# Masks on GpSimd, ReLU and sign on ScalarE, one VectorE operation for mask and maximum, in a planned graph-attention kernel

## The chip, the cores and the metric

The kernel runs on one core of a Trainium2 chip. A core has several engines that each work off their own instruction queue in order: TensorE (PE in the profile, its weight loads PEld), VectorE (DVE), ScalarE (ACT), GpSimd (POOL) and SyncE (SP); they meet through semaphores. 16 DMA engines move data between HBM and the on-chip memory SBUF; matmuls write to PSUM. The metric is the time of one execution in device microseconds (us).

## The reference, cut to what matters

```python
# x: 3327 x 1024, adj: 3327 x 3327 (0/1, symmetric, with the diagonal)
h = relu(layernorm(x))
f, g = h @ Wf + bf, h @ Wg + bg
e = relu(f @ g.T)
attention = softmax(where(adj > 0, e, -9e15), axis=1)
out = x + attention @ (h @ W + bW)
```

A node has about 16 neighbours and none has more than 37, so nearly all of the 3327 x 3327 scores are masked away.

## The kernel before, in words

The kernel never forms the whole score matrix. In its first part (to about 245 us) it normalises the rows of x and stores h in HBM (`hd`), makes one matrix A from Wf and Wg so that f·g of two nodes is (h A)·h', counts the neighbours of each node, lists them, and sorts the nodes by their number of neighbours. The second part, which the change touches, works through 26 tiles of 128 nodes, in the order `ORDER`. A tile of a given size gives each of its nodes the same number of neighbour slots (`CAPS`, 37 down to 11, 468 slots in all). A slot k of tile t is one row of 1024 floats for each of the 128 nodes, fetched from `hd` with an indirect DMA (512 KB) into one of 26 row buffers `G`.

The steps of a tile t have short names, which are the functions in the code:

- `L(t)`: fetch the lists of neighbours and the degree of the tile's nodes (POOL issues it). `G(t,k)`: fetch slot k (POOL). `H(t)`: fetch the tile's own h (POOL). `X`, `O`: add x to the result and scatter it to the output (POOL).
- `q`, `hT`, `hc`, `qc`, `fq`: transpose h, multiply with A on PE; ScalarE copies between PSUM and SBUF. The result `q` is 128 x 1026 wide; its column 1024 (`D`) is h·(Wf bg) plus a constant, the part of the score that the bias bg makes, here with its sign turned, since column D of `WgT` holds -bg (L899).
- `M(t)` (L1233): the mask: for 40 slots, -9e15 where the slot number is at or beyond the node's degree, else 0. One tensor_scalar of 128 x 40 on VectorE, into one of three buffers.
- `d(t,k)` (`dot`, L1258): multiply row k with q and sum it up: one score per node, one VectorE operation over 1024 elements.
- `S(t,c)` (`greatest`, L1265): for a chunk c of slots (tiles with more than 18 slots have two chunks, ten tiles do; 36 chunks in all): max(score, column D of q) plus the mask, in one scalar_tensor_tensor; then the negated maximum with a tensor_reduce into `nm`; for a second chunk also the minimum with the first chunk's `nm`.
- `E(t,c)`: exp(score + nm) with its sum, on ScalarE; `A(t)`: the factor that rescales the first chunk; `T`: the reciprocal of the sum (VectorE).
- `Y(t,c)`: scale row 0 (ScalarE). `s(t,k)`: row 0 += weight x row k on VectorE (L1313). For other slots, given by `SHARE`, `w(t,k)` scales the row on ScalarE (L1296) and `p(t,k)` adds it up on PE (L1300). `yt`, `yc`, `W`, `fo`, `rc`: transpose the weighted row on PE, multiply it with W, and copy the result out (L1316 to L1339).

The order of all these steps on every engine is fixed before the launch. `steps_of()` lists each step with its engine, two costs (how long it holds its engine, how long until its result is there) and the steps it must follow. `planned()` runs a list scheduler over that (`forward`), computes ranks backwards from the end (`backward`), adds random noise from `SEED` and `WIDE` to the ranks, repeats this 30 times and keeps the order with the least modelled end. The instructions are then issued in that order with no further reordering. So a change in one step's engine, cost or seed can move every other step. In this list a fetch holds POOL for 1.31 us, a dot holds VectorE for 1.148, an `s` step 1.205, the mask 0.16, and S 0.29 (first chunk) or 0.48 (second). A step of which several have an engine's turn is taken by least rank; a fetch also needs a free row buffer, which an earlier `s`, `p` or transpose has given back.

The list's dependence of `M(t)` on steps of tile t-3 is for the reuse of buffers; in the code the mask waits for the landing of `L(t)` and for S(t-3), which read the same mask buffer.

Of the kernel before, what the change touches and what calls it, by code (L numbers as in the profile page):

```python
# [12 lines left out]
AF = mybir.ActivationFunctionType  # L13
ALU = mybir.AluOpType
AX = mybir.AxisListType
# [23 lines left out]
TURNS = 6.0  # L39
ROWS = 26  # L40
PASSES = 30
SEED = 1
WIDE = 0.3
LAG = 2

# [283 lines left out]
def steps_of():  # L329

    steps = {}

    def add(engine, takes, lasts, name, *deps, **kw):
        steps[name] = Step(name, engine, takes, lasts, deps, **kw)

    chunks = [split(s) for s in ORDER]
    n = len(ORDER)
    add("DVE", 0.15, 0.2, ("fl", 0), at=265.0)
    for t, s in enumerate(ORDER):
        cap, ends = CAPS[s], chunks[t]  # L340
        add("POOL", 1.31, 1.31, ("L", t), ("M", t - 3), *(("G", t - 3, k) for k in range(CAPS[ORDER[t - 3]] if t > 2 else 0)))
        add("DMA", 0.4, 2.2, ("Ld", t), ("L", t))
        if t > 1:
            add("POOL", 1.31, 1.31, ("H", t), row=True)
            add("DMA", 1.33, 3.2, ("Hd", t), ("H", t))
            for g in range(2):
                add("PE", 0.44, 0.66, ("hT", t, g), ("Hd", t), ("hc", t - 1, g), ("hT", t, g - 1), frees=[("H", t)] * g)
            for g in range(2):
                add("ACT", 0.49, 0.6, ("hc", t, g), ("hT", t, g), *(("q", t - 1, i, j) for i in range(3) for j in range(QS)))
            for i in range(3):  # L350
                for j in range(QS):
                    add(
                        "PE", 4.66 / QS, 4.66 / QS + 0.2, ("q", t, i, j), ("hc", t, 0), ("hc", t, 1), ("fq", 3 * t + i),
                        ("q", t, i, j - 1),
                    )
                add(
                    "ACT", 0.4, 0.52, ("qc", t, i), ("q", t, i, QS - 1),
                    *(("d", t - 2, k) for k in range(CAPS[ORDER[t - 2]])), *(("S", t - 2, c) for c in range(2) if i == 2),
                )
                if 3 * t + i + 2 < 3 * n:  # L360
                    add("ACT", 0.38, 0.48, ("fq", 3 * t + i + 2), ("qc", t, i))
        used = [(op, t - 3, k) for op in "swY" for k in range(KM)]
        add("DVE", 0.16, 0.25, ("M", t), ("Ld", t), ("S", t - 3, 0), ("S", t - 3, 1), ("rc", t - 3, 0), ("rc", t - 3, 1), *used)
        if s < MORE:
            add("POOL", 1.31, 1.31, ("C", t), ("F", t - 1))
            add("DMA", 0.4, 2.5, ("Cd", t), ("C", t))
            add("DVE", 1.3, 1.4, ("F", t), ("Cd", t), *(("G", t - 1, k) for k in range(KL, CAPS[ORDER[t - 1]])))
        if t == n - 1:
            add("POOL", 1.31, 1.31, ("x", t), row=True)
            add("DMA", 1.33, 3.2, ("xd", t), ("x", t))  # L370
        summed, halves = [], ([], [])
        for c, (k0, k1) in enumerate(ends):
            last = c == len(ends) - 1
            for k in range(k0, k1):
                late = [("F", t)] if k >= KL else [("hc", 2, 1) if k < 6 else ("qc", 2, 1)] if t == 1 else []
                add("POOL", 1.31, 1.31, ("G", t, k), ("Ld", t), *late, row=True)
                add("DMA", 1.33, 3.2, ("Gd", t, k), ("G", t, k))
                add(
                    "DVE", 1.148, 1.32, ("d", t, k), ("Gd", t, k), *(("qc", t, i) for i in range(3)),
                    ("M", t), at=(256.0, 266.0)[t] if t < 2 else 0.0,  # L380
                )
            add("DVE", 0.48 if c else 0.29, 0.6 if c else 0.41, ("S", t, c), *(("d", t, k) for k in range(k0, k1)), ("M", t))
            if c:
                add("ACT", 0.28, 0.33, ("A", t), ("S", t, c))
            add("ACT", 0.48, 0.55, ("E", t, c), ("S", t, c), ("fl", t))
            if c:
                add("ACT", 1.05, 1.15, ("Y", t, c), ("A", t), *(("s", t, k) for k in range(1, k0)))
            else:
                add("ACT", 1.05, 1.15, ("Y", t, c), ("E", t, c))
            add("DVE", 0.25 * c + 0.11 * last + 0.01, 0.25 + 0.2 * c, ("T", t, c), ("E", t, c), *([("A", t)] if c else []))  # L390
            for k in range(max(k0, 1), k1):
                if k in on_tensor(t):
                    add("ACT", 1.05, 1.15, ("w", t, k), ("E", t, c))
                    add("PE", 0.873, 1.07, ("p", t, k), ("w", t, k), ("yc", t - 1, 0), ("yc", t - 1, 1), frees=[("G", t, k)])
                    summed.append(("p", t, k))
                elif t < n - 1:
                    add("DVE", 1.205, 1.29, ("s", t, k), ("E", t, c), ("Y", t, c), frees=[("G", t, k)])
                    summed.append(("s", t, k))
                else:
                    for g in range(2):  # L400
                        add("DVE", 0.66, 0.74, ("s", t, k, g), ("E", t, c), ("Y", t, c), ("s", t, k, g - 1), frees=[("G", t, k)] * g)
                        halves[g].append(("s", t, k, g))
        for o in range(2):
            add("ACT", 0.62, 0.72, ("fo", t, o), ("rc", t - 1, o), ("T", t, len(ends) - 1))
        for g in range(2):
            add(
                "PE", 0.44, 0.66, ("yt", t, g), *summed, *halves[g], ("Y", t, len(ends) - 1), ("yc", t - 1, 0), ("yc", t - 1, 1),
                ("yt", t, g - 1),
                frees=[("G", t, 0)] * g,
            )  # L410
        for g in range(2):
            add("ACT", 0.49, 0.6, ("yc", t, g), ("yt", t, g), *(("W", t - 1, o, j) for o in range(2) for j in range(WS)))
        for o in range(2):
            for j in range(WS):
                add(
                    "PE", 7.0 / WS, 7.0 / WS + 0.2, ("W", t, o, j), *(("yc", t, g) for g in range(2 * (j + 1) // WS)),
                    ("fo", t, o), ("W", t, o, j - 1),
                )
            if t < n - 1:
                add("ACT", 0.62, 0.72, ("rc", t, o), ("W", t, o, WS - 1), ("Od", t - 2))  # L420
            else:
                add("DVE", 0.6, 0.7, ("rc", t, o), ("W", t, o, WS - 1), ("Od", t - 2), ("xd", t), ("rc", t, o - 1), frees=[("x", t)] * o)
        if t < n - 1:
            add("POOL", 2.05, 2.05, ("X", t), ("rc", t, 0), ("rc", t, 1))
            add("DMA", 2.0, 4.5, ("Xd", t), ("X", t))
        add("POOL", 1.31, 1.31, ("O", t), ("Xd", t), ("rc", t, 0), ("rc", t, 1))
        add("DMA", 1.33, 3.2, ("Od", t), ("O", t))
    for step in steps.values():
        step.deps = [steps[d] for d in step.deps if d in steps]
        for d in step.deps:  # L430
            d.after.append(step)
    return list(steps.values())
# [147 lines left out]
def edge_path(ctx: ExitStack, tc: tile.TileContext, x, adj, Wf, bf, Wg, bg, W, bW, out, flag):  # L580
# [67 lines left out]
    with ExitStack() as part1:  # L648
# [212 lines left out]
        with tc.manual_schedule(engines={  # L861
# [34 lines left out]
            caps = c1.tile([P, NT], FP, name="caps")  # L896
            for j, cap in enumerate(CAPS):
                nc.gpsimd.memset(caps[:, j : j + 1], float(cap))
            nc.gpsimd.tensor_scalar(WgT[:, :, D], bgT, -1.0, None, op0=ALU.mult)  # L899
            load_adj(1)  # L900
            load_w(Wg, 0)
            load_w(Wg, 1)
# [265 lines left out]
    with tc.manual_schedule(engines={  # L1168
# [36 lines left out]
        def unit(of, t, c):  # L1205
            return of[2 * (t % 3) + c]
# [25 lines left out]

        def M(t):  # L1233
            degree = pis[t % 3].bitcast(FP)[:, KL : KL + 1]
            nc.vector.tensor_scalar(masks[t % 3], iotak, degree, NEG, op0=ALU.is_ge, op1=ALU.mult)

        def turned(t, g):
            for k in range(4):
# [25 lines left out]

        def greatest(t, c):  # L1265
            k0, k1 = chunks[t][c]
            sc, nm = scs[t % 3][:, k0:k1], unit(nms, t, c)
            nc.vector.scalar_tensor_tensor(  # L1268
                sc, sc, qs[t % 2][:, D : D + 1], masks[t % 3][:, k0:k1], op0=ALU.max, op1=ALU.add
            )  # L1270
            nc.vector.tensor_reduce(nm, sc, AX.X, ALU.max, negate=True)  # L1271
            if c:
                nc.vector.tensor_tensor(nm, nm, unit(nms, t, 0), op=ALU.min)

        def A(t):
            nc.scalar.activation(als[t % 3], unit(nms, t, 0), AF.Exp, bias=unit(nms, t, 1), scale=-1.0)
# [82 lines left out]
        def told(_):  # L1359
# [1 line left out]

        made = {
            "fl": told, "L": L, "H": H, "x": fetch_x, "C": C, "F": F, "G": fetch, "M": M, "hT": turned, "hc": hc, "q": third, "qc": qc,
            "fq": fq, "d": dot, "S": greatest, "A": A, "E": E, "Y": Y, "T": T, "w": w, "p": p, "s": s, "fo": fo, "yt": yt,
            "yc": yc, "W": project, "rc": rc, "X": X, "O": scatter,
        }
        plan = sorted(planned(ROWS, PASSES, SEED, WIDE)[1], key=lambda step: step[0])
# [45 lines left out]
```

## Time and profile before

| | us |
|---|---|
| median of 3 runs (1228.5 to 1233.57) | 1232.57 |
| the profiled execution | 1233.38 |
| its span, first to last instruction | 1231.6 |
| PE busy in the span | 1099.2 (89%) |
| VectorE busy | 1120.3 (91%) |
| ScalarE busy | 602.7 (49%) |
| GpSimd busy | 936.7 (76%) |
| mean granted TensorE clock | 0.963 of full |

The profile's groups name a line, an engine, the operation, what is written and read, the count, the busy time with the mean of one in ns, and the idle time of that engine just ahead of the group with what ended it. "issue" there is a gap in which the engine waited for nothing that the profile shows. A windows row gives each engine's busy time within a stretch of the span, with the number of instructions behind an x. A timeline row gives start, duration, engine, line and operation.

### The profile page before, as it was taken

How to read it: one execution, taken by the hardware profiler on the slowest of the kernel's cores; microseconds unless marked ns; L12 is line 12 of the kernel's file. 1: busy time of each engine (PE TensorE's matmuls, PEld its weight loads, DVE VectorE, ACT ScalarE, POOL GpSimd, SP SyncE). 2: the span in 40 equal slices, each digit the busy share in tenths (PEclk: the TensorE clock that was granted, in tenths of full speed). 3: DMA queues.
4: the chain of work that ended last, by engine and by line, in shares of the span. 5: the costliest groups of instructions: out<-in, count | busy, mean ns of one | idle time of the engine just before them, and what ended most of it. 6: DMA issues, size and time to landing. Idle time of an engine off the chain costs nothing. (4 is left out here: it accounts for less than half of the span.)

```text
span 1231.6 us, 14006 instructions
## 1 busy us (share of the span) xinstructions
PE 1099.2 (89%) x4508; PEld 697.5 (57%) x4508; DVE 1120.3 (91%) x2192; ACT 602.7 (49%) x924; POOL 936.7 (76%) x677
## 2 busy tenths in 40 slices
PE   2799990799939899999999999999899999999995
PEld 2566660466627466556655666665465656556553
DVE  5999998758898999998999999999999999999991
ACT  6899986324617355436452455443343333434240
POOL 8999996177676888878878778777887888787821
PEclk9899995799979999999999999999999999999998
DMA  9999999589788999989899899888998999998942
GB/s 370 420 396 397 393 359 324 191 313 350 270 257 281 329 314 315 319 285 339 302 342 308 307 306 320 279 286 299 317 294 288 311 310 321 283 316 256 324 118 54
DMA packets 101913, 374.43 MB, mean 304 GB/s; under 512 B 14859, under 2 KB 18602, under 8 KB 98631
## 3 DMA queue, kind: packets, MB, share of 16 engines
q0 software_dynamic: 79584, 286.77, 69.4%
q1 hardware_dynamic: 22246, 86.68, 18.7%
q8 instruction: 37, 0.61, 0.2%
q14 instruction: 46, 0.38, 0.1%
HBM read 344.11 MB, written 29.30 MB: 303 GB/s over the span
## 5 line engine op out<-in xcount | busy, mean ns | idle before, releaser
L639 POOL DMA_INDIRECT G<-hd,ps x454 | 567.4, 1250 | 159.2 <-issue 107.0
L1260 DVE CUSTOM_DVE_ANT_0 junk<-G,q 128x1024 bf16<-128x1024 f32 x468 | 563.9, 1224 | 34.0 <-DMA G<-hd,ps 19.2
L1328 PE MATMUL p_o<-W_sb,yT 128*128 128x512 f32 x832 | 365.8, 593 | 4.7 <-issue 3.1
L1313 DVE SCALAR_TENSOR_TENSOR G<-G,sc 128x1024 f32<-128x1024 f32 (+1 forms) x281 | 354.5, 1262 | 6.8 <-ACT G L1285 3.7
L1247 PE MATMUL p_q<-A_sb,hT 128*128 128x342 f32 x1152 | 350.5, 455 | 7.8 <-ACT p_q L1256 5.7
L1247 PEld LDWEIGHTS p_q<-A_sb,hT 128*128 128x128 f32 x1152 | 214.7, 191 | 116.4 <-issue 12.7
L1328 PEld LDWEIGHTS p_o<-W_sb,yT 128*128 128x128 f32 x832 | 155.1, 189 | 189.0 <-issue 180.9
L1300 PE MATMUL p_y<-ident,G 128*128 128x128 f32 x1552 | 190.1, 275 | 12.7 <-DVE G L1313 6.8
L1300 PEld LDWEIGHTS p_y<-ident,G 128*128 128x128 f32 x1552 | 175.0, 142 | 40.8 <-issue 15.3
L704 POOL TENSOR_TENSOR r<-r,iotaj 128x1664 f32<-128x1664 f32 (+3 forms) x50 | 183.9, 3750 | 3.9 <-ACT r L697 3.9
L1296 ACT ACTIVATE G<-G,sc 128x1024 f32<-128x1024 f32 x168 | 179.2, 1138 | 0.1
L837 PE MATMUL ps_A<-WgT,WfT 128*128 128x342 f32 x432 | 130.5, 461 | 1.6 <-ACT WfT L832 1.6
L767 DVE MAX8 cand<-r 128x8 f32<-128x208 f32 (+2 forms) x416 | 118.9, 360 | 4.0 <-POOL r L704 3.7
L1339 ACT ACTIVATE xp<-p_o,rs 128x512 f32<-128x512 f32 x50 | 34.2, 685 | 172.7 <-PE p_o L1328 131.5
L837 PEld LDWEIGHTS ps_A<-WgT,WfT 128*128 128x128 f32 x432 | 81.7, 193 | 42.1 <-issue 2.3
L697 ACT ACTIVATE r<-r 128x3327 f32<-128x3327 int32 (+3 forms) x27 | 77.3, 2865 | 10.2 <-DMA r<-in_adj_dram 10.2
L1253 ACT COPY q<-p_q 128x342 f32<-128x342 f32 x72 | 31.6, 443 | 103.0 <-PE p_q L1247 59.5
L1324 ACT COPY yT<-p_y 128x512 f32<-128x512 f32 x52 | 30.0, 587 | 71.6 <-PE p_y L1300 59.6
L1243 ACT COPY hT<-p_t 128x512 f32<-128x512 f32 x48 | 27.4, 585 | 74.4 <-PE p_t L1240 37.9
L639 POOL DMA_INDIRECT xp<-in_x_dram,perm x25 | 44.3, 1772 | 21.1 <-ACT xp L1339 14.4
L1281 ACT ACTIVATE sc<-sc,nm 128x10 f32<-128x10 f32 (+10 forms) x36 | 10.9, 304 | 94.4 <-DVE nm L1271 66.2
L1346 POOL DMA_INDIRECT out_dram<-xp,perm x25 | 32.8, 1310 | 31.1 <-DMA xp<-in_x_dram,perm 22.9
(148 smaller groups left out, 728.4 us busy)
## 6 DMA issues: line engine op xcount, KB each, us to landing
r<-in_adj_dram SPq DMA_DIRECT2D x24, 1663.5 KB, 12.8
xt<-in_x_dram SPq DMA_DIRECT2D x22, 512.0 KB, 13.6
hd<-xt SPq DMA_DIRECT2D x22, 512.0 KB, 10.5
G<-hd,ps POOLq DMA_INDIRECT x454
A_sb<-in_L_gnn_Wg_dram SPq DMA_DIRECT2D x8, 512.0 KB, 18.4
A_sb<-in_L_gnn_Wf_dram SPq DMA_DIRECT2D x8, 512.0 KB, 12.0
W_sb<-in_L_gnn_W_dram SPq DMA_DIRECT2D x8, 512.0 KB, 7.4
cd<-cand SPq DMA_DIRECT2D x25, 64.0 KB, 12.6
```

The lines of the kernel that those rows point to most:

```text
L639: return nc.gpsimd.indirect_dma_start(out=to, out_offset=None, in_=table, in_offset=bass.IndirectOffsetOnAxis(ap=idx, axis=0), **kw,)
L697: nc.scalar.activation(r[:n, b:e], a[:n, b:e], AF.Sign, accum_out=to)
L704: eng.tensor_mul(r[:n, b:e], r[:n, b:e], iotaj[:n, b:e])
L767: nc.vector.max(cands[t][:n, s * 8 : s * 8 + 8], r[:n, s * SW : min(N, (s + 1) * SW)])
L837: nc.tensor.matmul(ps[:, :QB], WfTs[c][:, k, :], WgT[:, k, o : o + QB], start=(k == 0), stop=(k == KD - 1))
L1247: nc.tensor.matmul(ps_q[(3 * t + i) % 2][:, :QB], hT[:, k, :], A_sb[:, k, i * QB : (i + 1) * QB], start=False, stop=(k == KD - 1), skip_gr ...
L1260: nc.vector.tensor_tensor_reduce(junks[k % 2], row(t, k), q[:, :D], 1.0, 0.0, op0=ALU.mult, op1=ALU.add, accum_out=scs[t % 3][:, k : k + 1],)
L1296: nc.scalar.activation(g, g, AF.Copy, scale=scs[t % 3][:, k : k + 1])
L1300: nc.tensor.matmul(ps_y[g][:, c, :], of[:, (4 * g + c) * P : (4 * g + c + 1) * P], ident, is_transpose=True, start=((t, g) not in begun an ...
L1313: nc.vector.scalar_tensor_tensor(y, row_k, scs[t % 3][:, k : k + 1], y, op0=ALU.mult, op1=ALU.add)
L1328: nc.tensor.matmul(ps_o[o], yT[:, k, :], W_sb[:, k, o * CB : (o + 1) * CB], start=False, stop=(k == KD - 1), skip_group_check=True,)
L1339: nc.scalar.activation(to, ps_o[o], AF.Copy, scale=rss[t % 3])
```

## The change

The mask moves to GpSimd's queue, with the same operation. The score's clamp is undone from S: a new step `R(t,c)` on ScalarE computes relu(score + column D of q) in place, for which column D of `WgT` holds +bg instead of -bg (all scores of a node differ from before by the same number, which softmax removes). S is then one tensor_tensor_reduce on VectorE: add the mask, write the sum, and take the maximum into `al` (first chunk) or `rs` (second chunk, where it starts from the first chunk's maximum in `al`). A new step `N(t,c)` on ScalarE writes the negated maximum to `nm`, which E and A read as before. The steps' list gets these engines, costs and dependences; the seed goes from 1 to 8, and the whole order of the second part is computed anew.

```diff
-SEED = 1
+SEED = 8
 ...
-                    *(("d", t - 2, k) for k in range(CAPS[ORDER[t - 2]])), *(("S", t - 2, c) for c in range(2) if i == 2),
+                    *(("d", t - 2, k) for k in range(CAPS[ORDER[t - 2]])), *(("R", t - 2, c) for c in range(2) if i == 2),
 ...
-        add("DVE", 0.16, 0.25, ("M", t), ("Ld", t), ("S", t - 3, 0), ("S", t - 3, 1), ("rc", t - 3, 0), ("rc", t - 3, 1), *used)
+        add("POOL", 0.2, 0.25, ("M", t), ("Ld", t), ("S", t - 3, 0), ("S", t - 3, 1), ("rc", t - 3, 0), ("rc", t - 3, 1), *used)
 ...
-            add("DVE", 0.48 if c else 0.29, 0.6 if c else 0.41, ("S", t, c), *(("d", t, k) for k in range(k0, k1)), ("M", t))
+            add("ACT", 0.2, 0.3, ("R", t, c), *(("d", t, k) for k in range(k0, k1)))
+            add("DVE", 0.22, 0.32, ("S", t, c), ("R", t, c), ("M", t), *([("S", t, 0)] if c else []))
+            add("ACT", 0.19, 0.28, ("N", t, c), ("S", t, c))
             if c:
-                add("ACT", 0.28, 0.33, ("A", t), ("S", t, c))
-            add("ACT", 0.48, 0.55, ("E", t, c), ("S", t, c), ("fl", t))
+                add("ACT", 0.28, 0.33, ("A", t), ("N", t, c), ("N", t, 0))
+            add("ACT", 0.48, 0.55, ("E", t, c), ("N", t, c), ("fl", t))
 ...
-            nc.gpsimd.tensor_scalar(WgT[:, :, D], bgT, -1.0, None, op0=ALU.mult)
+            nc.gpsimd.tensor_copy(WgT[:, :, D], bgT)
 ...
-            nc.vector.tensor_scalar(masks[t % 3], iotak, degree, NEG, op0=ALU.is_ge, op1=ALU.mult)
+            nc.gpsimd.tensor_scalar(masks[t % 3], iotak, degree, NEG, op0=ALU.is_ge, op1=ALU.mult)
 ...
         def greatest(t, c):
             k0, k1 = chunks[t][c]
-            sc, nm = scs[t % 3][:, k0:k1], unit(nms, t, c)
-            nc.vector.scalar_tensor_tensor(
-                sc, sc, qs[t % 2][:, D : D + 1], masks[t % 3][:, k0:k1], op0=ALU.max, op1=ALU.add
+            sc = scs[t % 3][:, k0:k1]
+            nc.vector.tensor_tensor_reduce(
+                sc, sc, masks[t % 3][:, k0:k1], 1.0, als[t % 3] if c else 0.0, op0=ALU.add, op1=ALU.max,
+                accum_out=(rss if c else als)[t % 3],
             )
-            nc.vector.tensor_reduce(nm, sc, AX.X, ALU.max, negate=True)
-            if c:
-                nc.vector.tensor_tensor(nm, nm, unit(nms, t, 0), op=ALU.min)
+
+        def negated(t, c):
+            nc.scalar.activation(unit(nms, t, c), (rss if c else als)[t % 3], AF.Copy, scale=-1.0)
+
+        def bounded(t, c):
+            k0, k1 = chunks[t][c]
+            sc = scs[t % 3][:, k0:k1]
+            nc.scalar.activation(sc, sc, AF.Relu, bias=qs[t % 2][:, D : D + 1])
```

More of the change, by code (lines that the diff above doesn't have):

```diff
@@ L1363, in edge_path @@
             "fl": told, "L": L, "H": H, "x": fetch_x, "C": C, "F": F, "G": fetch, "M": M, "hT": turned, "hc": hc, "q": third, "qc": qc,
-            "fq": fq, "d": dot, "S": greatest, "A": A, "E": E, "Y": Y, "T": T, "w": w, "p": p, "s": s, "fo": fo, "yt": yt,
+            "fq": fq, "d": dot, "R": bounded, "S": greatest, "N": negated, "A": A, "E": E, "Y": Y, "T": T, "w": w, "p": p, "s": s, "fo": fo, "yt": yt,
             "yc": yc, "W": project, "rc": rc, "X": X, "O": scatter,
```

## The prediction

> **What bounds the kernel now.** I first read the page's busy shares and its slices, because the shares say which engines can be the limit and the slices say where. This is the page:
>
> ```profile
> span 1231.6 us, 14006 instructions
> ...
> PE 1099.2 (89%) x4508; PEld 697.5 (57%) x4508; DVE 1120.3 (91%) x2192; ACT 602.7 (49%) x924; POOL 936.7 (76%) x677
> ...
> PE   2799990799939899999999999999899999999995
> ...
> DVE  5999998758898999998999999999999999999991
> ACT  6899986324617355436452455443343333434240
> POOL 8999996177676888878878778777887888787821
> ```
>
> VectorE and PE are near full from slice 14 to the end; ScalarE has more than half of its time free; POOL seems to have a quarter free. That last one is misleading, and the next two views say why. In the groups, the fetches of rows carry an idle time called "issue": 107.0 us over 454 fetches. In the timeline it is the same 0.30 us ahead of each fetch, so it is part of what a fetch costs. This is POOL in the stretch where the first dots begin (VectorE is idle until 253.48, then runs dots back to back until 261.5):
>
> ```profile
> 251.52 0.94 POOL L639 DMA_INDIRECT G<-hd,ps  x1 [0.30 <-issue]
> 252.76 0.94 POOL L639 DMA_INDIRECT G<-hd,ps  x1 [0.31 <-issue]
> 254.00 1.51 POOL L639 DMA_INDIRECT G<-hd,ps  x1 [0.30 <-issue]
> 255.82 1.99 POOL L639 DMA_INDIRECT G<-hd,ps  x1 [0.30 <-issue]
> 258.11 1.99 POOL L639 DMA_INDIRECT G<-hd,ps  x1 [0.30 <-issue]
> 260.40 1.98 POOL L639 DMA_INDIRECT G<-hd,ps  x1 [0.30 <-issue]
> 262.69 0.95 POOL L639 DMA_INDIRECT cts<-cd,perm  x1 [0.30 <-issue]
> ```
>
> A fetch takes 0.94 us beside an idle VectorE and up to 1.99 beside dots: it is stretched by about one VectorE operation (1.05). Over the run its mean is 1.25. So POOL's work in a window is its busy time plus 0.30 for each instruction. The windows (PE busy, PEld, DVE, ACT, POOL, then clock and DMA share):
>
> ```profile
> 400.00:520.00 120.00, 110.94 (x469) 69.37 (x468) 116.14 (x179) 57.36 (x90) 96.82 (x77) 0.99 0.93 319
> 520.00:880.00 360.00, 343.89 (x1491) 221.81 (x1490) 348.78 (x534) 164.62 (x257) 280.40 (x221) 0.99 0.91 309
> 880.00:1160.00 280.00, 276.90 (x1027) 165.44 (x1026) 275.18 (x392) 101.24 (x171) 222.37 (x169) 1.00 0.91 297
> ```
>
> POOL's spare time is 120 - 96.82 - 77 x 0.30 = 0.1 us in the first window, 360 - 280.40 - 66.3 = 13.3 in the second, 280 - 222.37 - 50.7 = 6.9 in the third: 20.3 us of 760. VectorE has 3.9, 11.2 and 4.8 us free, PE 9.1, 16.1 and 3.1. Three engines are within 3 or 4% of full at once. The chain that ended last shows who finishes late: it is nearly all PE from 1114 us on, with VectorE joining only through the last tile's steps (its half-width `s` steps end at 1202.80, and PE transposes their result from 1200.79 to 1204.44).
>
> **The change part by part.** Durations come from the profiled execution, so the sum is made against its 1233.38 us (span 1231.6 and 1.8 around it); that run is 0.8 above the median 1232.57. Less than 0.5%, 6.2 us, is about what a measurement of this kernel can't tell from no change.
>
> *Mask off VectorE.* 24 masks lie behind 250 us (two more at 244 are ahead of all dots). In the rows below the mask starts at 631.74 and the next dot at 631.94: it holds VectorE for 0.20; elsewhere the same difference is 0.15. 24 x 0.18 = 4.3 us less.
>
> *S shorter.* A second chunk's S, from its first row to the next `s` step, is 634.81 - 634.28 = 0.53 us; a first chunk's is 0.35 (614.82 to 615.17 in the timeline). 26 x 0.35 + 10 x 0.53 = 14.4 us now.
>
> ```profile
> 631.74 0.28 DVE L1235 TENSOR_SCALAR mask<-iotak,ps 128x40 f32<-128x40 f32 x1
> 631.94 1.21 DVE L1260 CUSTOM_DVE_ANT_0 junk<-G,q 128x1024 bf16<-128x1024 f32 x1
> 633.08 0.08 DVE L1260 DVE_READ_ACCUMULATOR2_ANT sc<- 128x1 f32 x1
> 633.08 1.27 DVE L1313 SCALAR_TENSOR_TENSOR G<-G,sc 128x1024 f32<-128x1024 f32 x1
> 634.28 0.22 DVE L1268 SCALAR_TENSOR_TENSOR sc<-sc,q,mask 128x10 f32<-128x10 f32 x1
> 634.53 0.16 DVE L1271 TENSOR_REDUCE nm<-sc 128x1 f32<-128x10 f32 x1
> 634.73 0.16 DVE L1273 TENSOR_TENSOR nm<-nm 128x1 f32<-128x1 f32 x1
> 634.81 1.28 DVE L1313 SCALAR_TENSOR_TENSOR G<-G,sc 128x1024 f32<-128x1024 f32 x1
> ```
>
> The new operation is the dot's kind on 10 to 19 elements, which no row has. The `s` step costs 1.289 at 1024 elements and 0.751 at 512, so 1.05 ns an element. Low: a dot holds VectorE for 1.15, less 1014 x 1.05 ns = 0.085. High: its duration 1.224 less the same 1.065 is 0.16, and its accumulator read 0.08 behind it, 0.24. I take 0.22, near the high end, since the small two-input row (L1268) is 0.22 itself. 36 x 0.22 = 7.9, so 6.5 us less (5.8 to 11.3). VectorE's relief in all: 4.3 + 6.5 = 10.8 us (10.1 to 15.6), spread evenly over the tiles between 275 and 1190 us, 66% of it (7.1) ahead of 880 us.
>
> *Mask on POOL.* Its own price has a row: the only small tensor_scalar on POOL (L899, 128x8) took 0.257 us, with VectorE not in its way. Between dots the trace shows none. Low end: the mask fills a piece of time in which the next fetch would only have been stretched (mean stretch 1.25 - 0.94 = 0.31), 0.26 - 0.31 = -0.05 each, -1 in all. High end: the mask is blocked by a dot (1.05) and pushes the next fetch into its long form (1.05): 0.26 + 2.10 = 2.36 each, 57 us. I take the mean stretch that the fetches show, 0.26 + 0.31 = 0.57, 24 x 0.57 = 13.7, since fetches are the nearest thing in that queue. Queued behind a mask are the fetches, and VectorE waits for these. Where POOL has spare time, this is hidden by it; it is not in 400 to 520 (three masks: 1.7 against 0.1 spare) nor in 560 to 640 (64.15 busy and 53 x 0.30 make 80.05 of 80; two masks, 1.1). There the fetches are just in time too: matching fetches with dots in the written order, the least time from the end of an issue to its dot is 3.3 to 5.8 us in tiles 2 to 7 and 4.7 to 5.4 in tiles 13 to 17, against 9.6 to 18 in tiles 9 to 12 and 22 to 25. So 1.6 + 1.1 = 2.7 us reach VectorE.
>
> *VectorE held by POOL's mask.* If POOL has to get in between two VectorE operations, VectorE's next one may wait for it: 0 to 0.26 each. No row bounds it better; I take the 0.26, since the stretched fetches show that the two engines exclude each other. 17 masks ahead of 880 us make 4.4, eight behind it 2.1.
>
> [...] No row here shows a mask on POOL beside a dot.
>
> *R and N on ScalarE.* R is like E's activation (128x10, 0.30 by the group L1281), N like the scaling of one column in the first part (0.20, L722 and L728): 36 x 0.50 = 18 us on an engine that is busy 16 of 40 us. Behind a waiting R or N on ScalarE stand E, the copies for PE (hc, qc, fq, yc, rc) and the w steps. ScalarE already stands waiting for S (66.2 + 13.1 us, in the waits), so the standing time mostly moves. The chain of a chunk gets longer: last dot, R 0.30, a hop, S 0.24, a hop, N 0.20, with hops of 0.1, against S 0.37 now: +0.57 us. In 30 of 36 chunks another VectorE operation already stands between the last dot and S, and can cover this. In six it does not (tiles 0, 19, 21, 23, 24, 25: S starts 0.04 us after the last dot ends), and five of them lie behind 880 us: 5 x 0.57 = 2.9 us of VectorE standing, of which the last tile's is on the end path directly.
>
> [...]
>
> *L899*, once in the first part, is the same size of operation on POOL: nothing, since it was hidden ahead of the first matmuls. *The new order*: unknown. It can only move waits, of which VectorE has 20 and PE 28 us between 400 and 1160; I give it 4 us either way and keep this in the range.
>
> *Sum.* Ahead of 880 us: -7.1 + 4.4 + 2.7 = 0.0. Behind it: -3.7 + 2.1 + 2.9 = +1.3. 1233.4 + 1.3 = 1234.7 for a run like the profiled one, 0.8 less for one like the median: **1234 us**, no change that can be told. Its own range is 1227 to 1239.
>
> **The rivals.**
>
> *The relief arrives whole.* The mask on POOL costs VectorE nothing and POOL less than its spare time. Then VectorE is 7.1 us ahead by 880 us, and PE has 9.1 + 16.1 us of idle time there to take it in; behind 880 PE has only 3.1 us free in 280, so no more than that can follow. 1233.4 - 10.2 = 1223. For: VectorE's 97% and PE's wait for `s` results (6.8 us at PE p_y). Against: POOL's 0.1 us of spare time from 400 to 520. Chance 0.27, 1215 to 1226.
>
> *POOL becomes the bound* (the other side). A mask costs POOL 0.26 and one stretch, 1.31 us: 24 x 1.31 = 31.4, less the 20.3 that are spare, 11 us more, with VectorE's relief turned into waits for rows: 1233.4 + 11.1 = 1245. It decides from (20.3 + 6.2) / 24 = 1.1 us per mask. For: the stretched fetches and the just-in-time leads. Against: the spare time, and that one stretch in two can be taken from the fetch behind. Chance 0.24, 1239 to 1260.
>
> *The longer chain is not covered.* If VectorE stands for 0.57 us at all 36 chunks, 20.5 less the relief 10.8 is 9.7 more: 1243. For: the rows of a tile are held longer, with only 26 buffers, so the next tile's dots may not be there as a cover. Against: the operation that stands between in 30 of 36 chunks. Chance 0.13.
>
> *The combined operation is no shorter than the pair* (the change doesn't do what it says): at 0.35 it saves only 10 x 0.18 + 4.3 = 6.1 us instead of 10.8, and the sum is 1238, still within no change.
>
> **How the numbers follow.** No change 0.36 (1227 to 1239), faster 0.27, slower 0.24 + 0.13 = 0.37. With the case of the relief cut at 1220 and the slow cases at 1251, about 0.1 is left out at each end.
>
> **What would show it.** S as one VectorE row of 0.16 with a read of 0.08, mean step to the next instruction 0.22; 24 masks on POOL after 250 us, of 0.26 if free and up to 1.3 if blocked; VectorE busy less by some 11 us; POOL's busy time plus 0.30 per fetch at 100% also in 520 to 880; VectorE's wait for rows (19.2 us for junk from G) up by 3 (up by more than 10 if POOL is the bound); dots behind a mask started late by 0.26; no table load after L1190. The prediction would be wrong if masks on POOL show 0.26 beside dots and the fetches behind them no longer, if the new order alone moves 10 us, or if ScalarE's standing at R and N delays PE's copies.

## The result and the profile after

The changed kernel takes 1270.45 us (median of 4 runs, 1267.6 to 1272.43) against 1233.07 before (the three runs of the table and a fourth of 1237.24): 1.031 of the time before, 95% interval 1.0277 to 1.0344. That is 37 us slower, where 1234 and a range up to 1251 were forecast. The profiled execution took 1268.92 us.

From the page of the changed kernel, the busy shares, the slices, and the groups of row fetches and dots:

```profile
span 1267.1 us, 14144 instructions
...
PE 1110.9 (88%) x4508; PEld 707.5 (56%) x4508; DVE 1109.4 (88%) x2156; ACT 619.0 (49%) x996; POOL 988.9 (78%) x703
...
PE   2799971898949998998999979899988997999995
...
DVE  5999997568998998998998978999989998898991
...
L641 POOL DMA_INDIRECT G<-hd,ps x454 | 589.6, 1299 | 145.0 <-issue 92.4
L1262 DVE CUSTOM_DVE_ANT_0 junk<-G,q 128x1024 bf16<-128x1024 f32 x468 | 565.0, 1223 | 63.9 <-DMA G<-hd,ps 44.6
```

The same two groups in the kernel before:

```profile
L639 POOL DMA_INDIRECT G<-hd,ps x454 | 567.4, 1250 | 159.2 <-issue 107.0
L1260 DVE CUSTOM_DVE_ANT_0 junk<-G,q 128x1024 bf16<-128x1024 f32 x468 | 563.9, 1224 | 34.0 <-DMA G<-hd,ps 19.2
```

VectorE was relieved of what the change meant to take: its busy time is 1109.4 us instead of 1120.3, 10.9 less. But it lost more than that to waits: 44.6 us ahead of dots for rows that had not landed, 19.2 before. A second wait is new: S stood for R on ScalarE. This is its row in the waits (total, times, longest):

```profile
DVE sc L1270 <- ACT sc L1281: 19.9, 11, 4.8
```

POOL's busy time is up by 52 us: 29.3 for the masks, 22 for the row fetches (mean 1.299 instead of 1.250). The windows (PE, PEld, DVE, ACT, POOL, clock, DMA share) show where this stands:

```profile
400.00:520.00 120.00, 112.71 (x486) 73.09 (x487) 113.51 (x174) 58.36 (x96) 97.92 (x76) 0.99 0.91 317
520.00:880.00 360.00, 337.67 (x1441) 218.73 (x1440) 332.20 (x507) 172.75 (x287) 289.99 (x223) 0.97 0.89 297
880.00:1160.00 280.00, 262.20 (x967) 157.99 (x966) 257.77 (x364) 98.62 (x176) 222.47 (x165) 0.97 0.86 279
```

PE has 6.2 us more idle time than before in the second window (22.3 against 16.1) and 14.7 more in the third (17.8 against 3.1); VectorE 16.6 and 17.4 more. Both engines that were full now wait for rows: VectorE for fetched ones, PE for those that ScalarE scales (23.0 us, 2.8 before). The lower granted clock in these windows is not the cause: on the chip of the first four runs below, the kernel before took 1233.5 us at 0.952 of the full clock, and the mask alone on GpSimd 1270.28 at 0.95. Nor are the transfers slower. The DMA share is below that of before, and from issue to landing a row takes 6.0 us (median) here, 6.2 in the run with the score's operations alone, which lost no time:

```profile
G<-hd,ps POOLq DMA_INDIRECT x454, 6.0
G<-hd,ps POOLq DMA_INDIRECT x454, 6.2
```

So the rows are issued late. Matching fetches with dots in the written order, the least time from the end of an issue to its dot is 3.4 to 4.7 us in 17 of the 26 tiles, all through the run. Before, it was 9.6 us or more in tiles 9 to 12 and 22 to 25: the lead that the fetches had there is gone. With the masks back on VectorE in the same new order (a run below), tiles 9 to 11 have 9.9 to 13.6 us again, where the changed kernel has 4.0 to 4.2.

The mask itself, in the changed kernel: first all masks, then POOL around one of them, then VectorE at the same time (start, duration, engine, line, operation).

```profile
L1237 POOL TENSOR_SCALAR mask<-iotak,ps x26: 418/1482/1774, 254.0 to 1210.2; 128x40 f32<-128x40 f32 x26
```

```profile
857.89 0.94 POOL L641 DMA_INDIRECT G<-hd,ps  x1 [0.30 <-ACT yT L1332]
858.91 1.59 POOL L1237 TENSOR_SCALAR mask<-iotak,ps 128x40 f32<-128x40 f32 x1
860.77 1.54 POOL L641 DMA_INDIRECT G<-hd,ps  x1 [0.27 <-issue]
...
857.85 1.29 DVE L1262 CUSTOM_DVE_ANT_0 junk<-G,q 128x1024 bf16<-128x1024 f32 x1
...
859.08 1.21 DVE L1262 CUSTOM_DVE_ANT_0 junk<-G,q 128x1024 bf16<-128x1024 f32 x1
...
860.22 1.22 DVE L1262 CUSTOM_DVE_ANT_0 junk<-G,q 128x1024 bf16<-128x1024 f32 x1
```

A mask beside an idle VectorE takes 0.42 us; half of them take 1.48 or more. The one shown starts 1.06 us into a dot, lasts over the whole next dot, and ends 0.28 us into the one behind that. So it takes in two ends of VectorE operations. From the end of the fetch ahead to the start of the fetch behind it are 1.94 us (0.30 without a mask), and that next fetch takes 1.54 us instead of the mean 1.25. It starts 0.55 us into a dot, the next dot starts 0.60 later, and the rest is 0.94, the time of a fetch beside an idle VectorE: it seems to wait for that seam. VectorE's dots follow each other in 1.23, 1.14 and 1.15 us: they are not held up at all.

Lateness in POOL's queue also comes back through ScalarE. `rc(t)` (L1347) may overwrite a result buffer only when the scatter of tile t-2, which POOL issues, has landed; when it is late, ScalarE stands, with all the copies for PE and R and N behind it. The total of these waits went from 24.9 us before to 94.9. The mask alone in the old order makes 67.1, so it does this by itself; but the new order with the masks on VectorE has 60.1, so the order has a large share too. This row of ScalarE is the longest of these waits:

```profile
757.20 1.27 ACT L1347 ACTIVATE xp<-p_o,rs 128x512 f32<-128x512 f32 x2 [17.70 <-DMA out_dram<-xp,perm]
```

Between tiles 11 and 12, where this wait lies, the changed kernel loses 12 us against the one before: the last dot of tile 11 is 5.7 us late, that of tile 12 17.7. The S of tile 11 stood 4.8 us for its R, which came behind this wait. With the masks back on VectorE in the new order the same place still loses 8.4 us, so most of this step is the order's and not the mask's.

### The profile page after: what moved, and what is told of

It is laid out like the page before. It is cut to its first block, busy times and chain, and to the rows that moved or that the text cites. A ratio compares the mean times of both kernels' runs of the same rounds, so it can differ in the third digit from the quotient of the medians.

```text
span 1267.1 us, 14144 instructions
## 1 busy us (share of the span) xinstructions
PE 1110.9 (88%) x4508; PEld 707.5 (56%) x4508; DVE 1109.4 (88%) x2156; ACT 619.0 (49%) x996; POOL 988.9 (78%) x703
## 5 line engine op out<-in xcount | busy, mean ns | idle before, releaser
L641 POOL DMA_INDIRECT G<-hd,ps x454 | 589.6, 1299 | 145.0 <-issue 92.4
L1262 DVE CUSTOM_DVE_ANT_0 junk<-G,q 128x1024 bf16<-128x1024 f32 x468 | 565.0, 1223 | 63.9 <-DMA G<-hd,ps 44.6
L1336 PE MATMUL p_o<-W_sb,yT 128*128 128x512 f32 x832 | 369.7, 597 | 1.7 <-ACT yT L1332 1.7
L1249 PEld LDWEIGHTS p_q<-A_sb,hT 128*128 128x128 f32 x1152 | 217.4, 193 | 116.1 <-issue 13.8
L1308 PE MATMUL p_y<-ident,G 128*128 128x128 f32 x1552 | 196.4, 280 | 29.9 <-ACT G L1304 23.0
L1308 PEld LDWEIGHTS p_y<-ident,G 128*128 128x128 f32 x1552 | 180.4, 145 | 63.0 <-ACT G L1304 30.3
L1347 ACT ACTIVATE xp<-p_o,rs 128x512 f32<-128x512 f32 x50 | 33.6, 685 | 207.1 <-DMA out_dram<-xp,perm 94.9
L1242 PE MATMUL p_t<-ident,G 128*128 128x128 f32 x192 | 31.2, 296 | 35.4 <-DMA G<-hd,perm 29.1
L641 POOL DMA_INDIRECT xp<-in_x_dram,perm x25 | 49.9, 1997 | 11.6 <-issue 5.8
L1354 POOL DMA_INDIRECT out_dram<-xp,perm x25 | 30.1, 1206 | 31.9 <-DMA xp<-in_x_dram,perm 22.7
## 6 DMA issues: line engine op xcount, KB each, us to landing
A_sb<-in_L_gnn_Wg_dram SPq DMA_DIRECT2D x8, 512.0 KB, 17.4
```

The costliest lines, as they stand in the source:

```text
L641: return nc.gpsimd.indirect_dma_start(out=to, out_offset=None, in_=table, in_offset=bass.IndirectOffsetOnAxis(ap=idx, axis=0), **kw,)
L1249: nc.tensor.matmul(ps_q[(3 * t + i) % 2][:, :QB], hT[:, k, :], A_sb[:, k, i * QB : (i + 1) * QB], start=False, stop=(k == KD - 1), skip_gr ...
L1262: nc.vector.tensor_tensor_reduce(junks[k % 2], row(t, k), q[:, :D], 1.0, 0.0, op0=ALU.mult, op1=ALU.add, accum_out=scs[t % 3][:, k : k + 1],)
L1308: nc.tensor.matmul(ps_y[g][:, c, :], of[:, (4 * g + c) * P : (4 * g + c + 1) * P], ident, is_transpose=True, start=((t, g) not in begun an ...
L1336: nc.tensor.matmul(ps_o[o], yT[:, k, :], W_sb[:, k, o * CB : (o + 1) * CB], start=False, stop=(k == KD - 1), skip_group_check=True,)
L1347: nc.scalar.activation(to, ps_o[o], AF.Copy, scale=rss[t % 3])
```

## The experiments

The change has three parts that can be told apart: the mask's engine, the score's operations, and the new order. The first four runs put them one by one into the order of the kernel before, which is possible since the order is a fixed list. Each ratio is against the kernel before on the same chip, with its 95% interval.

**The mask alone on GpSimd, in the old order.**

```diff
-            nc.vector.tensor_scalar(masks[t % 3], iotak, degree, NEG, op0=ALU.is_ge, op1=ALU.mult)
+            nc.gpsimd.tensor_scalar(masks[t % 3], iotak, degree, NEG, op0=ALU.is_ge, op1=ALU.mult)
```

> The order of the kernel before, with the mask's operation alone moved to GpSimd, at the same place of the written order. Three theories of the 37 us. Queue theory: a mask takes 1.1 us of its own and 0.4 of gap in POOL's queue, and the fetches behind it come late; 26 x 1.5 = 39 less the 20 us that POOL has spare, so 1245 to 1262. Chain theory (ReLU and sign on ScalarE make each chunk longer): nothing of that is here, 1228 to 1235. Order theory (the new order with seed 8 is worse by itself): 1228 to 1235 too.

Measured: 1270.59 us, ratio 1.0295 (1.0275 to 1.0315). This one line is as slow as the whole change. The chain and order theories fall; the queue theory had the cause, but its range ended at 1262, since it let all of POOL's 20 us of spare time take up the load. The masks of this run, and its group of dots:

```profile
L1235 POOL TENSOR_SCALAR mask<-iotak,ps x26: 425/1588/1933, 244.6 to 1204.4; 128x40 f32<-128x40 f32 x26
```

```profile
L1260 DVE CUSTOM_DVE_ANT_0 junk<-G,q 128x1024 bf16<-128x1024 f32 x468 | 565.2, 1223 | 65.5 <-DMA G<-hd,ps 49.9
```

The 23 masks behind 270 us all stand between two fetches. The hole between these is 1.59 us on average, 1.29 more than without a mask, and the fetch behind takes 1.58, 0.33 more than the mean: 1.62 us a mask, 39 us for the 24 behind 250. At the same 23 places the kernel before has a hole of 0.33 and a fetch of 1.27. POOL's true waits between 400 and 1160 us (gaps over the usual 0.30) fell only from 19.1 to 10.2 us, so the spare time took up 9 of the 39. The remaining 30 is near the 34.4 that the span grew by. Added up over POOL's whole queue, from the fetch ahead of the first of these masks to the end, the profiled run is 36.2 us longer than the one before: the holes at the masks make 30.7, the fetches behind them 7.2, and other fetches, which came out longer too, 11.4; the other holes are 13.1 shorter. What lengthened the other fetches is not settled.

**The score's operations alone, in the old order, mask on VectorE.** `bounded`, `greatest` and `negated` are those of the change.

```diff
-            nc.gpsimd.tensor_scalar(WgT[:, :, D], bgT, -1.0, None, op0=ALU.mult)
+            nc.gpsimd.tensor_copy(WgT[:, :, D], bgT)
 ...
+        def scored(t, c):
+            bounded(t, c)
+            greatest(t, c)
+            negated(t, c)
 ...
-            "S": greatest,
+            "S": scored,
```

> The order of the kernel before, with the mask on VectorE, and R, the new S and N issued one behind the other where S stood. Queue theory: no fetch is held up, VectorE gets some 6 us back and loses some at S waiting for R (36 x 0.3 at most): 1226 to 1238. Chain theory: 1243 or more. Order theory: 1226 to 1238.

Measured: 1230.94 us, ratio 0.998 (0.9948 to 1.0012): no change that can be told, as the queue and the order theory had it. The chain theory falls: S waits for R in this run too, 9 times and 7.7 us in all, and that costs no time that can be told. The rows of R and of S in this run (S without and with the start value):

```profile
L1279 ACT ACTIVATE sc<-sc,q x36: 296/306/323, 274.0 to 1190.1; 128x10 f32<-128x10 f32 x11, 128x15 f32<-128x15 f32 x4, 128x18 f32<-128x18 f32 x3, 128x13 f32<-128x13 f32 x3
...
L1268 DVE CUSTOM_DVE_ANT_0 sc<-sc,mask x26: 157/170/223, 274.4 to 1190.4; 128x10 f32<-128x10 f32 x9, 128x17 f32<-128x17 f32 x3, 128x15 f32<-128x15 f32 x3, 128x16 f32<-128x16 f32 x2
...
L1268 DVE CUSTOM_DVE_ANT_0 sc<-sc,mask,al x10: 218/227/268, 378.0 to 740.3; 128x11 f32<-128x11 f32 x2, 128x10 f32<-128x10 f32 x2, 128x9 f32<-128x9 f32 x2, 128x18 f32<-128x18 f32 x1
```

**Both edits in the old order**, that is the change without its new plan (the two diffs above together).

> The whole change but for the plan: both edits in the order of the kernel before. Queue theory: as the mask alone, 1245 to 1262. Chain theory: 1243 to 1255. Order theory: under 1242, and the rest up to 1270 comes only with the new order.

Measured: 1272.34 us, ratio 1.027 (1.0209 to 1.0332), the same as the mask alone within the intervals. The four runs spread from 1256.78 to 1277.29. The median is above the queue theory's 1262 (a ratio of 1.023, which lies within the interval) and the chain theory's 1255, and the order theory falls: nearly all of the loss is there without the new order.

**The new seed alone**, with the operations of before:

```diff
-SEED = 1
+SEED = 8
```

> The kernel before with the seed 8 alone, so another order of the same operations on the same engines. Order theory: the scatter between orders is large, 1250 to 1275. Queue and chain theories: within 8 us of the kernel before, 1226 to 1242.

Measured: 1245.88 us, ratio 1.0103 (1.0066 to 1.0139). This is 12 us, more than the queue theory's 8 and less than the order theory's 17, so neither had the size right: another order of the same work is worth about 1% by itself. In this run VectorE waits less for rows (14.3 us), but 15.9 us for scaled rows from ScalarE (11.8 at once); in the kernel before that was 2.7 us.

**The new order with the mask put back on VectorE** answers how much of the changed kernel's loss is its own order:

```diff
-            nc.gpsimd.tensor_scalar(masks[t % 3], iotak, degree, NEG, op0=ALU.is_ge, op1=ALU.mult)
+            nc.vector.tensor_scalar(masks[t % 3], iotak, degree, NEG, op0=ALU.is_ge, op1=ALU.mult)
```

> The changed kernel with its new order, with the mask alone put back on VectorE at the same place of the written order. Queue theory: the loss goes but for what the order itself costs, 1228 to 1248. If the new order was the cause as much as the mask: 1255 to 1268.

Measured: ratio 1.0125 (1.0021 to 1.023), 1253.94 us on a chip where the kernel before took 1242.01. In the terms of the expectation this is 1248 us, the upper end of the queue theory's range. So the new order costs something too, about 1% (0.2 to 2.3 by the interval). The mask on POOL makes 2.7 to 2.95% in the old order, and the whole change 3.1% with the order's own cost in it. Whether the two losses add up can't be told: with the order at 0.2% they would. That waits of a poor order vanish behind a queue that is late anyway would explain a smaller sum; no run shows it.

Next, what makes the mask slow on POOL: that it reads SBUF while VectorE does, or that anything stands between two fetches.

**A fill of 128x40 beside the masks.** From tile 5 on, 21 times, POOL fills unused floats; the masks stay on VectorE, and nothing reads what is filled.

```diff
             nc.vector.tensor_scalar(masks[t % 3], iotak, degree, NEG, op0=ALU.is_ge, op1=ALU.mult)
+            if t >= 5:
+                nc.gpsimd.memset(cts[0][:, :KM], 0.0)
```

> The kernel before, and from tile 5 on GpSimd also fills 128x40 unused floats with zero where the mask stands in the order (21 times); the masks stay on VectorE. The result is not touched by it. Lock theory (a mask on POOL reads SBUF, and waits for the end of a VectorE operation with two SBUF inputs): a fill reads nothing, so it takes 0.1 to 0.2 us and is not stretched; 1233 to 1241. Slot theory (any instruction between two fetches shifts them against VectorE's operations, and the next fetch comes out long): 21 x 1.0 or more, less the spare time: 1245 to 1258.

Measured: ratio 1.0026 (0.9977 to 1.0075). All fills of this run in one row:

```profile
L1237 POOL MEMSET cts<- x21: 146/147/739, 440.2 to 1195.7; 128x40 f32 x21
```

**A fill of 128x128**, otherwise the same (`nc.gpsimd.memset(cts[0], 0.0)`):

> As the run with the small fill, but 128x128, to hold POOL for about as long as a mask without contention does (0.2 to 0.3 us). Read-lock theory: nothing to wait for, a hole of 0.4 us at most and 1233 to 1242. Slot theory (it is the time held between two fetches that shifts them): the next fetches come out long, 1245 or more.

Measured: ratio 1.0019 (0.9993 to 1.0045).

```profile
L1237 POOL MEMSET cts<- x21: 218/223/827, 420.9 to 1167.0; 128x128 f32 x21
```

**A read of one column**, 128x1, in the same place:

```diff
+            if t >= 5:
+                nc.gpsimd.tensor_scalar(cts[0][:, :1], iotak[:, :1], 1.0, None, op0=ALU.mult)
```

> The kernel before, and from tile 5 on GpSimd also copies one column (128x1) of the slot numbers into unused space, 21 times where the mask stands; the masks stay on VectorE. Read-lock theory: its reading of SBUF alone makes it wait for the end of VectorE's operation, as the mask of 128x40 did, so the hole between two fetches is near 1.5 us (0.31 with a fill of 128x40), the next fetch is stretched too, and the time is 1250 to 1262. Size theory (the mask is slow because it is 40 elements of arithmetic): a hole of 0.3 to 0.6 and 1233 to 1242.

Measured: 1248.15 us, ratio 1.017 (1.0129 to 1.0212).

```profile
L1237 POOL TENSOR_SCALAR cts<-iotak x21: 362/441/1538, 420.1 to 1183.8; 128x1 f32<-128x1 f32 x21
```

Put together, from the timelines of POOL (holes are from the end of a fetch to the start of the next; 0.30 with nothing between; the cost of one is what the hole has over 0.30 and the next fetch over 1.25):

| between two fetches | hole, us | next fetch, us | cost of one, us | times | ratio |
|---|---|---|---|---|---|
| fill 128x40 | 0.36 | 1.33 | 0.14 | 21 | 1.0026 |
| fill 128x128 | 0.38 | 1.51 | 0.34 | 21 | 1.0019 |
| read and write 128x1 | 0.70 | 1.78 | 0.93 | 21 | 1.017 |
| mask 128x40 | 1.59 | 1.58 | 1.62 | 23 | 1.0295 |

The fills, which read nothing, are never held up but once (0.739 and 0.827), and cost nothing that can be told. A read of a single column is held: in 19 of 21 cases it ends 0.14 to 0.17 us behind the start of a VectorE operation, whatever its duration (0.36 to 1.15 us but for one), so it gets in at the seam between two of them. Its shortest hole is 0.55 us, so at least 0.15 of the 0.70 is holding. The larger part of its cost is the next fetch, which comes out long. No fill holds the queue for 0.55 us, so how much of the 1.7% a longer hole alone would make is not told apart. That the mask is held is plain from its own rows: 0.42 us beside an idle VectorE, most often 1.59 beside a busy one. The hole of 0.70 contradicts my number (near 1.5) but not the theory: one seam is enough for one column, the mask of 128x40 most often needs two (15 of the 24 behind 250 us). Why it needs two (more elements, or the pointer to the degree as a read of its own) is not settled. Nor does a run tell whether the two inputs matter that the lock theory names: the dots (`junk<-G,q`) and `s` steps here all have two. The size theory fails on the time (1.7% slower, where 1242, 0.7% over the time before, was the most expected of it), although the hole, 0.70, is nearer to its 0.3 to 0.6; the slot theory fails on the time of both fills, though the fetch behind the wide one is longer too (1.51). 21 x 0.93 = 20 us lies within the interval of the read's loss (16 to 26 us), but POOL's waits also shrank by 7 us there (19.1 to 12.0), so the sum is not closed.

**The mask twice on POOL.** The second copy goes to unused space, from tile 5 on.

```diff
-            nc.vector.tensor_scalar(masks[t % 3], iotak, degree, NEG, op0=ALU.is_ge, op1=ALU.mult)
+            nc.gpsimd.tensor_scalar(masks[t % 3], iotak, degree, NEG, op0=ALU.is_ge, op1=ALU.mult)
+            if t >= 5:
+                nc.gpsimd.tensor_scalar(cts[0][:, :KM], iotak, degree, NEG, op0=ALU.is_ge, op1=ALU.mult)
```

> The kernel with the mask alone on GpSimd in the old order (1270), and from tile 5 on each mask is computed a second time, into unused space (21 more). Queue theory: POOL has no spare time left, so each costs what it holds of the queue, 0.4 to 1.6 us: 1280 to 1300. If the 37 us were a matter of a few unlucky places in the order, the second copies would add little: 1268 to 1276.

Measured: 1296.0 us, ratio 1.0422 (1.0338 to 1.0507). Each further mask costs time: 1.3% for 21, or about 16 us (5 to 26 by the interval, if the first copies cost here what they cost alone). The rival's 1276, a ratio of 1.0345, is just inside the interval's lower end. At the 21 doubled masks the holes grew to 3.49 us, 1.88 more than with one mask, which would be 39 us. These holes are from the slowest of the five runs (1310.84 us), which is 43 us over the profiled run with single masks.

**The mask on ScalarE**, to free VectorE without POOL. Two activations make a limit that is large for valid slots and very negative for the others, and S takes the minimum with it:

```diff
-            nc.vector.tensor_scalar(masks[t % 3], iotak, degree, NEG, op0=ALU.is_ge, op1=ALU.mult)
+            nc.scalar.activation(lims[t % 3], degree, AF.Copy, scale=2.0**30, bias=-(2.0**29))
+            nc.scalar.activation(masks[t % 3], iotak, AF.Identity, scale=-(2.0**30), bias=lims[t % 3])
 ...
-                sc, sc, qs[t % 2][:, D : D + 1], masks[t % 3][:, k0:k1], op0=ALU.max, op1=ALU.add
+                sc, sc, qs[t % 2][:, D : D + 1], masks[t % 3][:, k0:k1], op0=ALU.max, op1=ALU.min
```

> The order of the kernel before; the mask is made on ScalarE, with two activations (a bias of 128x1, then a limit of 128x40 that S takes the minimum with, for the same result). VectorE is freed of the masks without any use of POOL. Queue theory: 4.3 us of relief at most, nothing lost in the fetches: 1226 to 1235. If POOL's mask were slow because the mask comes late for S, this, which is no earlier, would lose too: 1245 or more.

Measured: ratio 1.0031 (0.9987 to 1.0075); 1246.42 us where the kernel before took 1242.01. Nothing lost that can be told, and nothing won by VectorE's 4.3 us.

**Score and mask on ScalarE**, the change with all of VectorE's relief and none of POOL's load. The diff is against the run with the score's operations alone:

```diff
-            nc.vector.tensor_scalar(masks[t % 3], iotak, degree, NEG, op0=ALU.is_ge, op1=ALU.mult)
+            nc.scalar.activation(lims[t % 3], degree, AF.Copy, scale=-(2.0**30), bias=2.0**30)
+            nc.scalar.activation(masks[t % 3], iotak, AF.Relu, scale=2.0**30, bias=lims[t % 3])
 ...
-                sc, sc, masks[t % 3][:, k0:k1], 1.0, als[t % 3] if c else 0.0, op0=ALU.add, op1=ALU.max,
+                sc, sc, masks[t % 3][:, k0:k1], 1.0, als[t % 3] if c else 0.0, op0=ALU.subtract, op1=ALU.max,
```

> The change's score edit (ReLU and sign on ScalarE, one VectorE operation for mask and maximum) in the order of the kernel before, with the mask made on ScalarE as well, so that VectorE is freed of all that the change frees it of and POOL gets nothing. Queue theory: the change without its harm, 1224 to 1236. If the relief of VectorE were worth what it is long (10.8 us): 1223 or less.

Measured: 1235.18 us on a chip where the kernel before took 1228.94, ratio 1.0058 (1.0033 to 1.0084): 0.6% slower. The queue theory's 1236 is 0.2% over the time before, so no theory expected this loss; what causes it is open (beside R and N, ScalarE has two more activations per tile). In this order VectorE's relief wins nothing; an order planned for it was not run. Its windows:

```profile
400.00:520.00 120.00, 113.33 (x510) 73.12 (x509) 115.93 (x174) 63.64 (x109) 95.97 (x78) 1.00 0.94 326
520.00:880.00 360.00, 343.31 (x1458) 219.35 (x1457) 341.74 (x517) 172.05 (x303) 283.90 (x219) 0.99 0.89 305
880.00:1160.00 280.00, 276.04 (x1023) 164.96 (x1022) 271.52 (x382) 109.59 (x207) 224.97 (x169) 1.00 0.91 299
```

VectorE is busy 729.2 us between 400 and 1160 where it was 740.1 before, and PE 732.7 where it was 731.7: PE was as busy as before, and VectorE's relief became idle time. POOL's busy time is 604.8 (599.6 before).

No version that was run beats the kernel before: the best, the score's operations alone, can't be told from it.

## Why the prediction was wrong

The forecast was no change, 1234 us; the changed kernel took 1270.45. By the forecast's own steps:

- *What bounds the kernel*: right that POOL, VectorE and PE were all near full and that "issue" belongs to the fetch. The DMA engines, busy for 0.91 to 0.93 in the same rows, were not weighed; no run tells whether they are why VectorE's relief wins nothing. The spare time of POOL was read as if it could be used anywhere in its window; of about 20 us only 9 were used when the mask moved alone (19.1 to 10.2).
- *Mask off VectorE and S shorter*: right. 10.8 us was forecast, and VectorE's busy time fell by 10.9. In the changed kernel S is a row of 0.17 (0.26 with the start value, 0.23 in the run shown above) and a read of 0.08, against the 0.16 and 0.08 forecast.
- *Mask on POOL*: this is the step that failed. I priced a mask at its own 0.26 and the mean stretch of a fetch, 0.31, together 0.57 us and 13.7 in all. In the old order it held the queue for 1.29 us and stretched the fetch behind it by 0.33, 1.62 together and 39 in all. In the changed kernel, where fewer masks took in two ends of VectorE operations, the same reckoning gives 1.39 for each of the 26, 36 in all. The high end, 2.36, had both effects in it; I left it because fetches are the nearest row, but their mean contains the many that happen to fit (245 of the 454 take less than 0.95 us). Even free it is 0.42, not 0.26.
- *2.7 us of it reach VectorE*: too little, for the same reason. VectorE's wait for rows grew by 25 us in the changed kernel and by 31 with the mask alone.
- *VectorE held by POOL's mask*: wrong. The dots' mean is 1.223 us where it was 1.224, and with the mask alone on POOL the step from a dot beside a mask to the next operation is 1.169 us, 1.168 elsewhere. POOL waits for VectorE here, not the other way; the fetch rows that the 0.26 was argued from (0.94 to 1.99 us) show POOL's side alone. The 6.5 us of this term were not there; its 17 and 8 masks are also one too many (15 and 9).
- *R and N on ScalarE*: right in size (0.31 and 0.20), and the score's operations in the old order cost nothing that can be told (ratio 0.998). The two hops of the chain, taken as 0.1 us each without a row, show in the changed kernel as 0.14 or 0.15 from R to S (9 of the 11 times that S stood for R) and 0.03 or 0.04 from S to N (29 of 36). In the changed kernel the term came out larger: VectorE stood 19.9 us in S for R, where 2.9 was forecast; how much of this reached the end is not told apart. No table load follows: ScalarE's last ACT_TABLE_LOAD is the one at 267.87 us (L1192, 1.28 us long; L1190 at 267.26, also 1.28, in the kernel before), ahead of the first R at 276.94, and the 36 R and 36 E behind it show none.
- *The new order*: 4 us either way was too little. The seed alone is worth 1%, the new order with masks on VectorE 1.25% (0.2 to 2.3).
- *The rivals*: "POOL becomes the bound" was the right one, with its own point of decision: from 1.1 us per mask, and it measured 1.62. Its 1245 was too low because it took a mask at 1.31 and let the spare 20 us cover a part in full. "The relief arrives whole" had two errors: besides the mask on POOL, the last run shows no gain from the relief without it either. In the rival of the combined operation, the sum is 1239, not 1238.

## What to carry to other kernels

Before moving a small operation to an engine with a low busy share, count that engine's fixed gaps into its share (here 0.30 us ahead of each fetch), and ask whether its neighbours in the queue are timed against another engine: an operation that holds VectorE for 0.2 us cost 1.6 in this queue. Where a price lies between far ends, take the row that has the same access (here a read on POOL beside a busy VectorE), not the mean of a different one; where there is none, as in the profile before, keep the high end in the range. And when three engines are about equally full, relief of one may win nothing (here VectorE's 10.9 us), while a load on one of them (here POOL's 39 us) shows nearly in full; a reordered plan alone moved this kernel by 1%.

## What was not expected of the hardware

The GpSimd instruction that reads one column (128x1), placed between two fetches while VectorE was at its dots and `s` steps, took 0.44 us (median); in 19 of 21 cases it ended 0.14 to 0.17 us behind the start of a VectorE operation, so at the seam of two. The 128x40 mask, moved alone, most often took in two seams (15 of 24), with 1.59 us (median) against 0.42 beside an idle VectorE. Fills of 128x40 and 128x128 in the same places took 0.147 and 0.223 us (medians). VectorE lost no time to these masks that the rows show: from a dot beside one to the next operation it took 1.169 us, 1.168 elsewhere.
